# Macaron block in float32: turning the feed-forward tokens with VectorE's 32x32 blocks and DMAs by way of DRAM instead of TensorE transposes

## The chip, the cores and the metric

The kernel runs on one core of a Trainium2 chip. Its time is the device time of one execution in microseconds, given as the median of several runs. Profiles are of one execution, taken by the hardware profiler. The engines are TensorE (PE, with its weight loads PEld), VectorE (DVE), ScalarE (ACT), GpSimd (POOL) and SyncE (SP, which here only issues DMAs). Each engine works through its own instructions in program order and waits on semaphores for the others.

## The reference

```python
def reference(x, Wq, Wk, Wv, Wo, w1, b1, w2, b2):        # x: 16 x 256 x 256, float32
    x = x + 0.5 * ffn(layernorm(x), w1, b1, w2, b2)
    x = x + attention(layernorm(x), Wq, Wk, Wv, Wo)       # 16 heads of 16, rotary, causal
    x = x + 0.5 * ffn(layernorm(x), w1, b1, w2, b2)
    return x

def ffn(x, w1, b1, w2, b2):                               # 256 -> 1024 -> 256
    h = gelu(x @ bit_quant(w1).T + b1)                    # exact GELU
    return h @ bit_quant(w2).T + b2                       # bit_quant: round(w / mean|w|) to -1, 0, 1
```

## The kernel before

The 4096 tokens stay on the chip in eight tiles `x_0` to `x_7`, each a block of 512 tokens: 128 partitions, four tokens on each (`BT = 4`), 256 features. The program has three parts: the first feed-forward (`ln == 0`), the attention, whose first steps begin beside the first feed-forward's last blocks (`head`), and the last feed-forward (`ln == 2`), which begins beside the attention's end. Both feed-forwards are made by `ffn(ln, after)`.

A feed-forward works in 64 steps, `u = 8 i + f`, for block `i` and eighth `f` of the 1024 hidden features. Step `(i, f)` does `up(i, f)`: four matmuls of 512 columns into a PSUM tile `m`, two with the high part of the normalized tokens (`xnT[i][0]`) and then two with the rest (`xnT[i][1]`), each for two halves `k` of the 256 features. ScalarE then makes the GELU of `m` twice, once rounded to the matmul's format (`h_high`) and once whole (`h_whole`), and the difference `h_rest` is taken by GpSimd for f = 1, 3, 5 and by VectorE otherwise. The second product, `down`, is two steps behind (`LATE = 2`): step `u` ends with `down` of step `u - 2`, eight matmuls into a PSUM tile `w`, which want `h_high` and `h_rest` of that step. So after `up(i, 2)` TensorE does `down(i, 0)`, `up(i, 3)`, `down(i, 1)`, `up(i, 4)`, `down(i, 2)`. After a block's last `down` VectorE adds the product to `x` in two halves (this falls into step 1 of the next block); in the last feed-forward SP then stores the block.

The next block's tokens are made ready in between. `stats` takes mean and variance of the tokens of block `i + 2` on VectorE in steps 4 to 7, `finish_stats` makes `rstd` of them on GpSimd behind step 7. `prepare(i + 1)` in step 3 normalizes the next block's four token groups on VectorE into `xn`, of which there is one buffer. `turn_in(i + 1, k)` in steps 5 and 6 transposes them on TensorE, four 128x128 transposes per half `k` into a PSUM tile `mm`; ScalarE copies that to the high part, and VectorE subtracts it from the PSUM tile to get the rest. `add_bias(i)` in step 6 adds the output bias to `x_i` on GpSimd. In the first feed-forward, statistics for the attention's norm (`later`) are spread over the steps of the next block.

The order of every engine's instructions is the order in which the program writes them: the wrapper `InOrder` keeps it, so nothing is reordered by a planner. In the profile almost all instructions carry that wrapper's line, L172, so tiles tell them apart: `m` is up's product, `w` down's, `mm` what else goes through PSUM, `xnT` both the high part and the rest. `flat1` and `flat2` hold the raw weights `w1` and `w2` at first; later the attention's rotary step uses `flat1` and the first half of `flat2`.

Of the kernel before, what the change touches and what calls it, by code (L numbers as in the profile page):

```python
# [8 lines left out]
FP = mybir.dt.float32  # L9
FR = mybir.dt.float32r  # L10
AF = mybir.ActivationFunctionType
# [4 lines left out]
P = 128  # L16
D = 256
KC = D // P
FF = 1024
# [10 lines left out]
def kernel(  # L30
# [17 lines left out]
    BT = 4  # L48
    TB = BT * P
    NBLK = NT // TB  # L50
# [24 lines left out]
    b1_sb = const.tile([P, NFC], FP, name="b1_sb")  # L75
# [5 lines left out]
    flat1, flat2 = (state.tile([P, 2 * FF], FP, name=f"w_{n}") for n in range(2))  # L81
# [19 lines left out]
    for k in range(KC):  # L101
        rows = slice(k * P, (k + 1) * P)
        nc.sync.dma_start(out=wv[:, k, :], in_=wqkvT[rows, 2 * D :])
        for at in range(0, 2 * D, 4 * HD):
            n, j, e = at // D, at // P % 2, at // (4 * HD) % 2
            nc.sync.dma_start(
                out=wqk[:, k, n, j, :, e, :],
                in_=wqkvT[rows, at : at + 4 * HD].rearrange("p (r d) -> p r d", d=HD),
            )
    for at in range(0, P, HD):  # L110
        r, n = at // 32, at // HD % 2
        nc.sync.dma_start(
            out=wo[at : at + HD, :, :],
            in_=woT.rearrange("(k n r d) f -> n r d k f", n=2, r=4, d=HD)[n, r],
# [19 lines left out]
        out=mask_k,  # L134
        in_=mask_k,
# [28 lines left out]
    class InOrder:  # L164
# [11 lines left out]
    tensor, vector, scalar, gpsimd, sync = (  # L176
        InOrder(engine) for engine in (nc.tensor, nc.vector, nc.scalar, nc.gpsimd, nc.sync)
    )
# [4 lines left out]
    def stats(ln, n):  # L183
        st = small.tile([P, 6], FP, name="st")
        vector.bn_stats(st, tokens(n))
        vector.bn_aggr(mv[ln][:, n, :], st)

    def finish_stats(ln, first, n):

        var = small.tile([P, BT], FP, name="var")  # L190
        gpsimd.tensor_scalar(
            var[:, 0:n], mv[ln][:, first : first + n, 1], LN_EPS, 1.0, ALU.add, ALU.mult
        )
        gpsimd.tensor_tensor(
            rstd[ln][:, first : first + n], var[:, 0:n], power[:, 0:n], ALU.pow
        )

    def normalize(ln, n, to, engine=None):
        (engine or vector).tensor_scalar(
            to,  # L200
            tokens(n),
            mv[ln][:, n, 0:1],
            rstd[ln][:, n : n + 1],
            ALU.subtract,
            ALU.mult,
        )
# [68 lines left out]

    LATE = 2

    def ffn(ln, after):
        xn, xnT, hT, ys = {}, {}, {}, {}

        def measure(i):
            if ln == 0:
                for t in range(BT):
                    stats(0, i * BT + t)
                finish_stats(0, i * BT, BT)

        def prepare(i, engine=None):
            xn[i] = fp.tile([P, BT, D], FP, name="xn", bufs=1)
            for t in range(BT):
                normalize(ln, i * BT + t, xn[i][:, t, :], engine)  # L290
            xnT[i] = [fp.tile([P, KC, TB], FR, name=f"xnT_{n}") for n in range(2)]

        def add_bias(i):
            gpsimd.tensor_add(xs[i], xs[i], b2_sb.unsqueeze(1).to_broadcast([P, BT, D]))

        def turn_in(i, k):
            tp = ps_mm.tile([P, TB], FP, name="mm")
            for t in range(BT):
                tensor.transpose(
                    tp[:, t * P : (t + 1) * P], xn[i][:, t, k * P : (k + 1) * P], ident  # L300
                )
            high, rest = (xnT[i][n][:, k, :] for n in range(2))
            scalar.copy(high, tp)
            return lambda: vector.tensor_sub(rest, tp, high.bitcast(FP))

        first = {}

        def up_first(i, f, to=None):
            h = first[i, f] = ps_m.tile([P, TB], FP, name="m") if to is None else to
            for n in range(2):  # L310
                for k in range(KC):
                    tensor.matmul(
                        h,
                        w1q[:, k, f * P : (f + 1) * P],
                        xnT[i][n][:, k, :],
                        start=(n == 0 and k == 0),
                        stop=(n == 1 and k == KC - 1),
                    )

        def up(i, f):  # L320
            if (i, f) not in first:
                up_first(i, f)
            h = first.pop((i, f))
            high = fp.tile([P, TB], FR, name="h_high", bufs=LATE + 3)
            rest = fp.tile([P, TB], FR, name="h_rest", bufs=LATE + 3)
            whole = fp.tile([P, TB], FP, name="h_whole", bufs=3)
            scalar.activation(high, h, AF.Gelu, bias=b1_sb[:, f : f + 1])
            scalar.activation(whole, h, AF.Gelu, bias=b1_sb[:, f : f + 1])

            engine = gpsimd if f in (1, 3, 5) and not (ln == 0 and i == NBLK - 1) else vector  # L330
            engine.tensor_sub(rest, whole, high.bitcast(FP))
            hT[i, f] = (high, rest)

        def down(i, f):
            if f == 0 and ln == 2 and i == NBLK - 1:

                ys[i] = [ps_mm.tile([P, 2, D], FP, name="mm") for t in range(0, BT, 2)]
            elif f == 0:
                y = ps_w.tile([P, BT, D], FP, name="w")
                ys[i] = [y[:, t : t + 2, :] for t in range(0, BT, 2)]  # L340
            parts = hT.pop((i, f))
            order = [(t, n) for t in range(BT) for n in range(2)]
            if ln == 2 and (i, f) == (NBLK - 1, NFC - 1):

                order = [(t, n) for n in range(2) for t in range(BT)]
            for t, n in order:

                tensor.matmul(
                    ys[i][t // 2][:, t % 2, :],
                    parts[n][:, t * P : (t + 1) * P],  # L350
                    w2q[:, f, :],
                    start=(f == 0 and n == 0 and t % 2 == 0),
                    stop=(f == NFC - 1 and n == 1 and t % 2 == 1),
                )
            if f == NFC - 1:
                for t in range(0, BT, 2):
                    xt = xs[i][:, t : t + 2, :]
                    vector.scalar_tensor_tensor(
                        xt, ys[i][t // 2], 0.5, xt, ALU.mult, ALU.add
                    )  # L360
                for t in range(0, BT, 2):
                    after(i, t)

        def begin():
            measure(0)
            if ln == 0:
                sizes(0)
            prepare(0)
            if ln == 0:
                threshold(0)  # L370
                signs(0, lambda w: w[:, :, 0 : FF // 2])
            for k in range(KC):
                turn_in(0, k)()
            if ln == 0:
                signs(0, lambda w: w[:, :, FF // 2 :])
                sizes(1)

        def step(u):
            i, f = divmod(u, NFC)
            if i < NBLK:  # L380
                up(i, f)
                if ln == 0 and u == 0:
                    threshold(1)
                if ln == 0 and u in (0, 3):
                    part = slice(0, NFC // 2) if u == 0 else slice(NFC // 2, NFC)
                    signs(1, lambda w: w[:, part, :])
                if ln == 0 and u == 4:
                    gpsimd.tensor_scalar(b2_sb, b2_sb, 0.5, 0.0, ALU.mult, ALU.add)
                if u == 1:
                    measure(1)  # L390
                if f >= 4 and i + 2 < NBLK:
                    stats(ln, (i + 2) * BT + f - 4)
                    if f == NFC - 1:
                        finish_stats(ln, (i + 2) * BT, BT)
                if i + 1 < NBLK and (ln, i) != (2, 0):
                    if f == 3:
                        prepare(i + 1)
                    if f in (5, 6):
                        turn_in(i + 1, f - 5)()
                if f == (1 if i == NBLK - 1 else 6):  # L400
                    add_bias(i)
            if u >= LATE:
                down(*divmod(u - LATE, NFC))
            if ln == 0 and u == 2 * NFC + 2:
                make_tables()
            if ln == 0 and u < (NBLK - 1) * NFC and later:
                later.pop(0)()

        return begin, step, prepare, turn_in, up_first
# [14 lines left out]
    xn_a, xnT, qT, kT, o, oT, y_a = {}, {}, {}, {}, {}, {}, {}  # L424
# [307 lines left out]


    begin, step, prepare, turn_in, up_first = ffn(2, store)
    rest = []
    for p in range(8):
# [7 lines left out]
        rest = made  # L744
        if p == 0:
            prepare(0, gpsimd)
    a, z = NB - 2, NB - 1
# [84 lines left out]
```

## Time and profile before

| What | Value |
|---|---|
| Time, median of 3 runs | 620.18 us (618.72 to 620.56) |
| The profiled execution's own time | 619.01 us |
| Its span | 617.2 us |
| Granted TensorE clock | 0.999 |
| Busy: PE, DVE, ACT, POOL | 592.9, 475.6, 391.5, 322.2 us |
| DMA engines, mean over the span | 34 GB/s |
| First feed-forward | from about 8 to 141 us |
| Last feed-forward, steps | from about 480 us to the end |

The span is the profiled execution without what lies around it, some 1.8 us. Busy times are of this one execution; a matmul's end is modelled, so a busy PE is not PE at its peak. A line of the chain of waits gives start, duration and what the chain went through; a line of a timeline gives start, duration, engine, source line, operation, output and inputs with their shapes, and in brackets the idle time before it and who ended it.

### The profile page before, as it was taken

The page shows a single profiled execution, that of the slowest core. Times are in us where ns is not written, and L with a number is a line of the kernel's source. Part 1 is how long each engine was busy: PE and PEld are TensorE (multiplying, and loading weights), DVE is VectorE, ACT ScalarE, POOL GpSimd, SP SyncE. Part 2 cuts the span into 40 slices and gives each one's busy share as a digit, 9 for nine tenths or more (in the row PEclk, how much of TensorE's full clock was granted, in tenths as well). Part 3 has the DMA queues.
Part 4 walks back from the last instruction along what each step waited for, and adds up shares of the span by engine and source line. Part 5 has one row for each costly group of instructions (what it writes and reads, how often), then busy time and mean ns, then how long its engine had stood idle before and what let it go on. Part 6 is the DMA issues. An engine that isn't in the chain of part 4 may idle for free.

```text
span 617.2 us, 14403 instructions
## 1 busy us (share of the span) xinstructions
PE 592.9 (96%) x5388; PEld 471.5 (76%) x5388; DVE 475.6 (77%) x1682; ACT 391.5 (63%) x668; POOL 322.2 (52%) x297
## 2 busy tenths in 40 slices
PE   4999999999999999999999999999999999999997
PEld 3798989887667777777777777777766788888886
DVE  6877887786788888888889888888896466666653
ACT  4667666764576666565666666666665666666674
POOL 3655555682465556555665467453822354444443
PEclk9999999999999999999999999999999999999999
DMA  8810000000001001100010001100000011110001
GB/s 290 176 23 1 2 1 19 17 1 18 19 37 37 20 20 37 37 29 28 19 38 36 21 19 37 37 20 21 36 4 2 2 35 35 35 35 34 30 20 55
DMA packets 25589, 21.28 MB, mean 34 GB/s; under 512 B 11056, under 2 KB 21168, under 8 KB 25520
## 3 DMA queue, kind: packets, MB, share of 16 engines
q1 hardware_dynamic: 24960, 19.44, 9.9%
q8 instruction: 43, 0.70, 0.5%
q10 hardware_dynamic: 560, 0.92, 0.4%
q14 instruction: 26, 0.21, 0.1%
HBM read 7.51 MB, written 4.19 MB: 19 GB/s over the span
## 4 chain that ended last, share of the span: by engine, by line
PE 78%; DVE 12%; ACT 6%; issue 2%; DMA 1%; POOL 1%; DVEq 0%; SPq 0%; ACTq 0%; POOLq 0%
PE mm L172 29%; PE w L172 26%; PE m L172 23%; DVE masked L172 3%; DVE h_rest L172 2%; ACT pT L172 2%; DVE w L172 2%; ACT h_high L172 1%; ACT h_whole L172 1%; DMA w<-in_w1T_dram 1%; DVE xn L172 1%; DVE st L172 1%; DVE xnT L172 1%; DVE w2q L172 1%; DVE x L172 0%
## 5 line engine op out<-in xcount | busy, mean ns | idle before, releaser
L172 DVE CUSTOM_DVE_ANT_0 masked<-m,mask_q 128x128 f32<-128x128 f32 x480 | 141.8, 350 | 32.5 <-PE m L172 31.2
L172 PE MATMUL m<-xnT,w1q 128*128 128x512 f32 x504 | 142.5, 403 | 3.5 <-DVE xnT L172 2.7
L172 ACT ACTIVATE pT<-w 128x768 f32<-128x768 f32 x128 | 103.9, 812 | 65.9 <-DVE w L172 60.2
L172 ACT ACTIVATE h_high<-m,b_sb 128x512 fp32r<-128x512 f32 x126 | 86.8, 689 | 81.6 <-PE m L172 81.5
L172 PE MATMUL w<-qT,kT 32*128 32x256 f32 (+1 forms) x1024 | 126.3, 351 | 3.5 <-ACT pT L172 2.0
L172 DVE TENSOR_TENSOR h_rest<-h_whole,h_high 128x512 fp32r<-128x512 f32 x83 | 75.2, 908 | 68.0 <-ACT h_whole L172 67.7
L172 PE MATMUL m<-kT,qT 32*128 32x128 f32 x960 | 124.6, 352 | 0.7 <-ACT kT L172 0.7
L172 PEld LDWEIGHTS w<-qT,kT 32*128 32x128 f32 x1024 | 92.7, 184 | 38.4 <-issue 28.6
L172 PE MATMUL w<-w2q,h_high 128*128 128x256 f32 x480 | 120.8, 286 | 1.0 <-DVE w2q L172 1.0
L172 PE MATMUL w<-w2q,h_rest 128*128 128x256 f32 x480 | 118.1, 280 | 0.8 <-POOL h_rest L172 0.7
L172 POOL TENSOR_TENSOR h_rest<-h_whole,h_high 128x512 fp32r<-128x512 f32 x45 | 60.2, 1339 | 90.4 <-ACT h_whole L172 90.2
L172 PEld LDWEIGHTS m<-xnT,w1q 128*128 128x128 f32 x504 | 86.8, 190 | 19.1 <-DVE xnT L172 5.5
L172 PEld LDWEIGHTS w<-w2q,h_rest 128*128 128x128 f32 x480 | 90.6, 189 | 5.8 <-POOL h_rest L172 1.2
L172 PEld LDWEIGHTS w<-w2q,h_high 128*128 128x128 f32 x480 | 90.3, 188 | 5.6 <-DVE w2q L172 1.4
L172 DVE TENSOR_TENSOR w<-w,mask_k 128x512 f32<-128x512 f32 x128 | 88.9, 695 | 4.2 <-PE w L172 4.1
L172 ACT ACTIVATE h_whole<-m,b_sb 128x512 f32<-128x512 f32 x126 | 85.8, 681 | 0.0
L172 PEld LDWEIGHTS m<-kT,qT 32*128 32x128 f32 x960 | 73.2, 185 | 5.9 <-DVE maxes L172 4.1
L172 POOL TENSOR_TENSOR o<-avs,inv 128x256 f32<-128x256 f32 x32 | 20.3, 636 | 97.0 <-DVE inv L172 97.0
L172 PE MATMUL mm<-xnT_a,wqk 128*128 128x256 f32 x256 | 63.5, 391 | 0.0
L172 POOL TENSOR_TENSOR w<-w,cosT 128x512 f32<-128x512 f32 x32 | 41.3, 1289 | 30.0 <-ACT w L172 16.0
L172 POOL TENSOR_TENSOR w<-w,sinT 128x512 f32<-128x512 f32 x32 | 40.9, 1277 | 27.8 <-DMA w<-w 27.7
L172 PEld LDWEIGHTS mm<-xnT_a,wqk 128*128 128x128 f32 x256 | 46.1, 190 | 11.4 <-PE m L172 4.6
(86 smaller groups left out, 875.1 us busy)
## 6 DMA issues: line engine op xcount, KB each, us to landing
w<-w SPq DMA_DIRECT2D x64, 128.0 KB
out_dram<-x SPq DMA_DIRECT2D x15, 256.0 KB
x<-in_x_dram SPq DMA_DIRECT2D x7, 512.0 KB
w<-in_w2T_dram SPq DMA_DIRECT2D x1, 1024.0 KB
qT<-mT SPq DMA_DIRECT2D x64, 4.0 KB
w<-in_w1T_dram SPq DMA_DIRECT2D x1, 512.0 KB
w<-in_w1T_dram ACTq DMA_DIRECT2D x1, 512.0 KB
wqk<-in_wqkvT_dram SPq DMA_DIRECT2D x16, 32.0 KB
```

The lines of the kernel that those rows point to most:

```text
L172: return tc.keep_in_program_order(getattr(self.engine, name)(*args, **kwargs))
```

## The change

For blocks 2 to 7 of both feed-forwards (`by_blocks`) the tokens are no longer transposed on TensorE. `prepare` is moved from step 3 of the block before to its step 0. It normalizes as before, then VectorE transposes the block's 128x1024 values in 32x32 squares into `turned`, the second half of `flat2`; SP writes that to a DRAM tile of 512 KB (two buffers) and reads it back in four DMAs of 128 KB, each to 32 partitions of the rest's buffer `xnT[i][1]`, in pieces of 512 bytes. In step 6 `turn_in` copies both halves to the high part on ScalarE, out of SBUF, and then VectorE subtracts the high part from the rest in place.

The tokens of such a block stand in another order in the transposed layout. The GELU puts them back: its input is read in the new order and its two outputs are written in the old one, in runs of 32 columns.

`stats` and `finish_stats` of steps 4 to 7 are written behind `prepare` and `turn_in` in the step, no longer ahead of them. Block 1 is turned as before.

```diff
+    turned = flat2[:, FF:]
+    dram = ctx.enter_context(
+        tc.tile_pool(name="rows", bufs=2, space=bass.MemoryType.DRAM)
+    )
     def ffn(ln, after):
         xn, xnT, hT, ys = {}, {}, {}, {}
+        by_blocks = range(2, NBLK)
...
             xnT[i] = [fp.tile([P, KC, TB], FR, name=f"xnT_{n}") for n in range(2)]
+            if i in by_blocks:
+                vector.transpose(turned, xn[i].rearrange("p n (j t) -> p j n t", t=32))
+                rows = dram.tile([P, 2 * TB], FP, name="rows")
+                sync.dma_start(out=rows, in_=turned)
+                of = rows.rearrange("(a f) (k j q) -> j f k a q", a=4, k=KC, j=4)
+                for j in range(4):
+                    sync.dma_start(
+                        out=xnT[i][1][32 * j : 32 * j + 32]
+                        .bitcast(FP)
+                        .rearrange("p k (a q) -> p k a q", a=4),
+                        in_=of[j],
+                    )
...
         def turn_in(i, k):
+            if i in by_blocks:
+                high, rest = (xnT[i][n][:, k, :] for n in range(2))
+                scalar.copy(high, rest.bitcast(FP))
+                return lambda: vector.tensor_sub(rest, rest.bitcast(FP), high.bitcast(FP))
...
-            scalar.activation(high, h, AF.Gelu, bias=b1_sb[:, f : f + 1])
-            scalar.activation(whole, h, AF.Gelu, bias=b1_sb[:, f : f + 1])
+            for to in (high, whole):
+                if i in by_blocks:
+                    to = to.rearrange("p (n a t) -> p a n t", n=BT, a=4)
+                    of = h.rearrange("p (a n t) -> p a n t", n=BT, a=4)
+                else:
+                    of = h
+                scalar.activation(to, of, AF.Gelu, bias=b1_sb[:, f : f + 1])
...
                 if u == 1:
                     measure(1)
+                if i + 1 < NBLK and (ln, i) != (2, 0):
+                    early = i + 1 in by_blocks
+                    if f == (0 if early else 3):
+                        prepare(i + 1)
+                    if early and f == 6:
+                        for rests in [turn_in(i + 1, k) for k in range(KC)]:
+                            rests()
+                    if not early and f in (5, 6):
+                        turn_in(i + 1, f - 5)()
                 if f >= 4 and i + 2 < NBLK:
                     stats(ln, (i + 2) * BT + f - 4)
                     if f == NFC - 1:
                         finish_stats(ln, (i + 2) * BT, BT)
-                if i + 1 < NBLK and (ln, i) != (2, 0):
-                    if f == 3:
-                        prepare(i + 1)
-                    if f in (5, 6):
-                        turn_in(i + 1, f - 5)()
```

## The prediction

> **What bounds the kernel now.** I read the page first, then TensorE's share by stage, then the chain of waits over one block, then the timelines of VectorE (DVE) and GpSimd (POOL) beside it, then the spread of single durations by tile. "up" is the four matmuls of a step into `m`, "down" the eight into `w`.
>
> ```profile
> PE 592.9 (96%) x5388; PEld 471.5 (76%) x5388; DVE 475.6 (77%) x1682; ACT 391.5 (63%) x668; POOL 322.2 (52%) x297
> ```
> The stages (us, then busy us per engine), one block each, from the first feed-forward (FFN) and from the last:
> ```profile
> 63.21:79.01 15.80, 15.80 (x106) 14.27 (x105) 12.67 (x30) 11.08 (x19) 9.54 (x9) 1.00 0.01 2
> 528.78:545.41 16.63, 16.09 (x107) 14.20 (x106) 10.54 (x22) 11.09 (x19) 7.47 (x6) 1.00 0.10 33
> ```
> TensorE is all there is in the first; in the last it lacks 0.54 us a block. The chain over that block's end (start, us, what) shows why:
> ```profile
> 523.39 0.44 PE mm L172 x4
> 523.83 0.94 PE w L172 x8
> 524.77 0.94 PE m L172 x4
> ...
> 525.74 0.69 ACT h_high L172
> 526.42 0.59 ACT h_whole L172
> ...
> 527.04 1.96 DVE h_rest L172
> 528.99 0.35 DVE st L172
> ...
> 529.55 0.59 DVE xnT L172
> ...
> 530.18 0.50 PE m L172
> ```
> A step is 0.93 + 0.94 = 1.87 us, eight are 14.95; the two groups of four transposes (`mm`) add 0.88, the wait 0.5 to 0.8. The 1.96 us `h_rest` is what the prediction turns on. In the timeline:
> ```profile
> 526.02 2.42 POOL L172 TENSOR_TENSOR x<-x,b_sb 128x1024 f32<-128x1024 f32 x1
> ...
> 527.04 1.96 DVE L172 TENSOR_TENSOR h_rest<-h_whole,h_high 128x512 fp32r<-128x512 f32 x1 [1.14 <-ACT h_whole L172]
> ...
> 529.46 0.66 DVE L172 TENSOR_TENSOR xnT<-mm,xnT 128x512 fp32r<-128x512 f32 x1
> ```
> DVE's difference of two SBUF tiles stands still until POOL's bias add ends (528.44) and then needs 0.57 more. By tile (ns, min/median/max):
> ```profile
> L172 DVE TENSOR_TENSOR h_rest<-h_whole,h_high x83: 658/693/2843, 15.1 to 611.2; 128x512 fp32r<-128x512 f32 x83
> ...
> L172 DVE TENSOR_TENSOR xnT<-mm,xnT x32: 652/658/692, 11.5 to 595.4; 128x512 fp32r<-128x512 f32 x32
> ...
> L172 DVE STREAM_TRANSPOSE oT<-o x32: 433/435/446, 181.6 to 486.8; 128x256 f32<-128x256 f32 x32
> ```
> The same subtraction with one operand in PSUM (`xnT<-mm`) was never held, at most 692 ns. Normalizations (SBUF to SBUF) are held too; here the four of a block in DVE's timeline, and in POOL's the work among them:
> ```profile
> 70.53 2.33 DVE L172 TENSOR_SCALAR xn<-x,mv,rstd 128x256 f32<-128x256 f32 x4
> ```
> ```profile
> 71.28 1.43 POOL L172 TENSOR_TENSOR h_rest<-h_whole,h_high 128x512 fp32r<-128x512 f32 x1 [2.44 <-ACT h_whole L172]
> ```
> Undisturbed the four take 1.38 (as at 536.36); POOL cut in ahead of the last one, which waited out the whole 1.3 us.
>
> **What is removed.** 2 x 4 transposes on TensorE in twelve block ends (blocks 2 to 7 of both FFNs): 0.88 each. If nothing else were late, all blocks would go to 14.95: 0.86 off 15.81 in the first FFN, 1.66 off 16.61 in the last.
>
> **What is added.** (a) DVE: one 128x1024 block transpose per block. `oT` (256 columns) takes 0.435, `avs` (512, out of PSUM) 0.707, so 1.06 ns a column: 1.25 us; between 0.9 (if the fixed part is larger) and 1.5 (if the 32-column runs cost), I take 1.25. None of the 32 `oT` was held (446 ns at most), so I take it as free of POOL. (b) Each rest is now SBUF minus SBUF: 0.60 as before, but now open to POOL's hold. (c) ACT's copy reads SBUF, 0.59 as from PSUM (`vals`, written in strided runs, takes 372 ns and the plain `mT` 371, so the turned GELU output costs nothing; bounds 0 and 0.1, hidden in ACT's 0.6 us idle per step). (d) SP: five DMAs. The wait for the first one's landing stands ahead of the stores, which nobody awaits, and in blocks 5 and 6 ahead of the rotary pairs.
>
> The trip: two stores of 256 KB give the price, SP's timeline first, then what the DMA engines moved in slices of 0.1 us from 534 on.
> ```profile
> 534.31 0.97 SPq L728 DMA_DIRECT2D out_dram<-x  x2
> ```
> ```profile
> GB/s 0 0 0 0 0 0 0 0 0 0 0 0 236 358 369 317 287 338 379 328 338 348 358 348 358 358 348 154 21 0 0 0 0 0 0 0 0 0 0 0
> ```
> First byte 0.9 after issue, 512 KB in 1.5, and 0.4 until the semaphore is acted on (a rotary pair's last data at 157.05 released POOL at 157.54): 2.8 us out. Back: four issues at 0.5 (bounds 0.37, a store, and 0.95, the `wqk` loads), 0.5 to the last one's first byte, 0.4 of data, 0.45 to act: 3.35. Together 6.1; with the dear issues 8. The 64-byte pieces of `wqk` moved at some 60 GB/s (8.7 us for 512 KB), which sets the upper end at 15; 512-byte pieces lie nearer to the store's 1 KB. The Trainium skill ("DMA: Bandwidth & Descriptors", Anatomy of one DMA) puts about 2 us of fixed cost on each DMA, most of it the write receipt, longest towards HBM; an estimate by that is 3.2 out and 4.7 back, 7.9. No row here shows a store's receipt that long, and the sum below would not change.
>
> **The timetable of a changed block, last FFN.** Zero is the end of up(i,0). An `h_rest` can start 1.33 after its up (530.68 to 532.01). DVE's r1, the second rest, ends 0.55 before zero (530.13 to 530.68). Behind it now come statistics 0.53, h_rest(7) 0.60, statistics 0.53: 1.11. `var` and `rstd` on POOL take 1.39 (531.27 to 532.66): 2.50. h_rest(0) is done at 1.93, so the normalizations, moved to step 0, wait for rstd, start at 2.55, and meet POOL's h_rest(1), ready at 1.87 + 1.33 = 3.20: two pass, POOL runs to 4.54, two follow to 5.20. Block transpose to 6.4. The residual adds of the block before (2 x 0.60) stand behind it: 7.6. Then h_rest(2) meets POOL's h_rest(3) (5.61 + 1.33 = 6.94, to 8.23) and ends at 8.23 + 0.57 = 8.80. TensorE wants it for down(2) at 4 x 1.87 = 7.48: a new wait of 1.37, where before DVE had 0.9 us of idle time in front of it.
>
> Everything behind moves by 1.37: h_rest(5) on POOL from 9.35 + 1.37 + 1.33 = 12.05 to 13.3, the bias add to 15.7. h_rest(6), ready at 11.22 + 1.37 + 1.33 = 13.92, is held to 15.7 and ends at 16.3; two rests make 17.5; plus 0.55 the next zero is 18.04. Without this second wait it would be 14.95 + 1.37 = 16.32. So 18.04 against 16.61. The trip isn't in it: transposed at 6.4, landed at 12.5; DVE wants the copies from 16.3 on, so landing may be 3 us later.
>
> **First FFN.** The same up to 8.80 (one statistics more fits under POOL's hold). `rstd` of the attention norm stands ahead of the bias add, which asks at 13.3 + 1.4 = 14.7. DVE does h_rest(6) 13.92 to 14.52 and r0 to 15.15; POOL, waiting, goes next (as in the rows at 71.28) until 17.57; r1 ends 18.14, zero at 18.69 against 15.81: +2.9. If r1 came first the block would be about 16.4, but h_rest(7) would be held instead, and rstd would reach the next block at +4.3, which lengthens the wait at down(2) to 2.0: 16.4 to 18.7 are the bounds. Blocks 5 and 6 run beside the attention's first steps. In block 5 TensorE has 4.8 us of projections between its steps, under which both waits mostly fit: +0.5 (bounds -0.9, +2.9). In block 6 the rotary products on POOL meet the normalizations (already 3.4 us of chain there, 123.62): +2.8 (bounds -0.9, +5).
>
> The Trainium skill ("VectorE: DVE Perf Modes", What auto-detection actually checks) lets an op with one SBUF source use both ports; the `oT` rows show neither that speed nor a hold. By that rule the block transpose would take some 0.7, as an estimate, and h_rest(2) behind it would still be held to 8.80.
>
> **Sum.** First FFN 4 x 2.9 + 0.5 + 2.8 = 14.9. Last FFN: its first changed block takes 16.02 now, so 2.0, then 5 x 1.43 = 7.2: 9.2. Together +24.1. The profiled execution took 619.01 (span 617.2), 1.2 under the median of 620.18; on the median, 644.
>
> **Rivals.**
> (1) The hold doesn't reach the new forms, or POOL's bias add comes after all three differences, and nothing stalls: 4 x 0.86 + 0.9 + 1.5 in the first FFN, 1.07 + 5 x 1.66 in the last, 15 off: 604. Its place is step 6; it decides if the bias add asks after r1 has started, 0.4 us later than in the first FFN's undelayed order (9.35 + 1.33 + 1.3 + 1.4 = 13.4) and 1.8 later in the last. For it: 0.9 us of idle DVE before h_rest(2) today. Against it: every bias add in the last FFN's rows holds h_rest(6).
> (2) The four normalizations keep POOL out, so the wait at down(2) vanishes (transposed at 5.1, h_rest(2) at 6.9, before POOL asks) and only the bias add costs: last FFN 14.95 + 1.4 = 16.35 (-1.0 in sum), first FFN about 17.3 (+6.9 with blocks 5 and 6): 626. Against it: the 2.33 row.
> (3) The trip is the limit: from landing later than 15.5 on, each us is one per block. At the 64-byte rate landing is near 19: up to 3.8 x 12 on top, half of it likelier: 667.
>
> **Chances.** Forecast 0.66, (2) 0.15, (3) 0.09, (1) and mixtures that come out faster 0.10. A measurement here tells 0.3% (1.9 us) from no change; of (2), 0.03 lies within that. So faster 0.10, same 0.03, slower 0.87. The range leaves out (1) and (3): from 621, the low end of (2), to 662, the forecast with block 6 at +5, block 5 at +2.9 and half a us more in each block and wait.
>
> **What would show it.** Right: in the last FFN's blocks a period near 18.0 with two gaps on TensorE, before down(2) on `h_rest` and before up(i+1,0) on `xnT`; `xnT` differences on DVE with maxima above 1.5 us; `rstd` about 2.5 after zero; copies on ACT not waiting for DMA. Wrong: `xnT<-xnT` never over 0.75 us (then 1), blocks with one gap only (2), or ACT's copies released by a DMA (3).

## The result and the profile after

The changed kernel takes 648.37 us (median of 4 runs, 647.78 to 649.25) against 619.62 us before (618.72 to 620.56): the ratio is 1.0465, 95% interval 1.0443 to 1.0487. The prediction was 644 (621 to 662), so the direction, the size and most of the mechanism held; the first feed-forward cost more than forecast.

The profiled execution has a span of 646.9 us (before 617.2), 29.7 more. First the page's line of busy times, the granted clock in tenths, and the chain that ended last, by engine:

```profile
PE 595.4 (92%) x5292; PEld 467.5 (72%) x5292; DVE 510.1 (79%) x1694; ACT 393.1 (61%) x668; POOL 323.7 (50%) x297
...
PEclk9998989889999999999999999999999999999999
...
PE 56%; DVE 22%; DMA 6%; ACT 5%; issue 5%; POOL 3%; SPq 2%; DVEq 0%; ACTq 0%; POOLq 0%
```

TensorE has 96 instructions fewer and is nevertheless busy 2.5 us longer. One part of that is its clock, which was halved for a while in the first feed-forward (the 8s in the clock's row; more on that at the end). Another is that a block broken up by waits shows more busy time even at full clock: 15.87 us in the last feed-forward's row below, against 14.93 where nothing waits (e9). It was on 78% of the chain before and is on 56% now. VectorE's busy time grew by 34.5 us: twelve block transposes are 15 of that, and most of the rest is operations that stand still while GpSimd works. The page's groups say what TensorE waited for (after the bars: busy us, mean ns of one, then idle us just before them and what ended most of it):

```profile
L172 PE MATMUL m<-xnT,w1q 128*128 128x512 f32 x504 | 151.0, 415 | 16.3 <-DVE xnT L172 14.2
...
L172 PE MATMUL w<-w2q,h_rest 128*128 128x256 f32 x480 | 121.8, 286 | 16.1 <-DVE h_rest L172 14.6
```

Before, those two idle times were 3.5 and 0.8 us. These are the two waits the prediction named: the next block's tokens (`xnT`) before `up(i+1, 0)`, and `h_rest` before `down`. One block of each feed-forward in the view by stages (columns as in the prediction's):

```profile
551.00:569.25 18.25, 15.87 (x97) 13.41 (x96) 13.47 (x23) 10.98 (x19) 7.83 (x7) 1.00 0.26 88
64.00:83.00 19.00, 15.65 (x100) 13.57 (x99) 15.50 (x32) 11.16 (x19) 9.52 (x9) 1.00 0.17 56
```

The periods, from one block's fourth matmul of `up(i, 0)` to the next block's, tell where the 29.7 us are. In the table, block i's period is the one in which block i + 1 is made ready, so the change acts on blocks 1 to 6:

| Block | 1 | 2 | 3 | 4 | 5 | 6 | sum |
|---|---|---|---|---|---|---|---|
| First FFN, before | 15.81 | 16.87 | 15.81 | 15.82 | 20.61 | 17.19 | 102.1 |
| First FFN, after | 17.13 | 19.17 | 18.99 | 18.96 | 24.04 | 23.30 | 121.6 |
| Last FFN, before | 16.72 | 16.61 | 16.62 | 16.62 | 16.61 | 16.08 | 99.3 |
| Last FFN, after | 18.34 | 18.24 | 18.24 | 18.21 | 18.25 | 18.25 | 109.5 |

That is +19.5 and +10.3, together the whole difference of the spans. VectorE's timeline over one block of the last feed-forward, with GpSimd's beside it, shows both waits being made (start, duration, operation; in brackets the idle time before it):

```profile
549.19 2.37 DVE L172 TENSOR_TENSOR h_rest<-h_whole,h_high 128x512 fp32r<-128x512 f32 x1 [3.52 <-ACT h_whole L172]
551.48 1.28 DVE L172 TENSOR_TENSOR xnT<-xnT,xnT 128x512 fp32r<-128x512 f32 x2
...
556.26 2.40 DVE L172 TENSOR_SCALAR xn<-x,mv,rstd 128x256 f32<-128x256 f32 x4 [0.91 <-POOL rstd L172]
558.70 1.25 DVE L172 STREAM_TRANSPOSE w<-xn 128x1024 f32<-128x1024 f32 x1
559.87 1.25 DVE L172 SCALAR_TENSOR_TENSOR x<-w,x 128x512 f32<-128x512 f32 x2
561.04 1.79 DVE L172 TENSOR_TENSOR h_rest<-h_whole,h_high 128x512 fp32r<-128x512 f32 x2
```
```profile
548.61 2.40 POOL L172 TENSOR_TENSOR x<-x,b_sb 128x1024 f32<-128x1024 f32 x1
554.55 0.20 POOL L172 TENSOR_SCALAR var<-mv 128x4 f32<-128x4 f32 x1 [3.54 <-DVE mv L172]
554.83 1.40 POOL L172 TENSOR_TENSOR rstd<-var,power 128x4 f32<-128x4 f32 x1
556.58 1.30 POOL L172 TENSOR_TENSOR h_rest<-h_whole,h_high 128x512 fp32r<-128x512 f32 x1 [0.35 <-ACT h_whole L172]
560.32 1.28 POOL L172 TENSOR_TENSOR h_rest<-h_whole,h_high 128x512 fp32r<-128x512 f32 x1 [2.45 <-ACT h_whole L172]
```

(The block transpose's target `turned` carries the name `w` in the trace, after the weights that lay there first.) At 549.19 `h_rest(6)` stands still until GpSimd's bias add ends at 551.01, then needs 0.55, and only then do the two rests of `xnT` follow: the wait at the block's end. From 556.26 on, the normalizations, the block transpose and the residual adds are one queue, and it is itself lengthened by a hold: the four normalizations take 2.40 us where four undisturbed ones took 1.38, with GpSimd's `h_rest(1)` (556.58) among them; `h_rest(2)` begins behind it at 561.04, is held by GpSimd's `h_rest(3)` to 561.60 and reaches TensorE at 562.2: the wait before `down(i, 2)`. In TensorE's row of steps the first wait makes a step of 3.41 out of 1.87 (1.54 lost), the second 3.50 (1.63 lost).

### The profile page after: what moved, and what is told of

It is laid out like the page before. It is cut to its first block, busy times and chain, and to the rows that moved or that the text cites. A ratio compares the mean times of both kernels' runs of the same rounds, so it can differ in the third digit from the quotient of the medians.

```text
span 646.9 us, 14484 instructions
## 1 busy us (share of the span) xinstructions
PE 595.4 (92%) x5292; PEld 467.5 (72%) x5292; DVE 510.1 (79%) x1694; ACT 393.1 (61%) x668; POOL 323.7 (50%) x297
## 4 chain that ended last, share of the span: by engine, by line
PE 56%; DVE 22%; DMA 6%; ACT 5%; issue 5%; POOL 3%; SPq 2%; DVEq 0%; ACTq 0%; POOLq 0%
PE mm L172 26%; PE w L172 17%; PE m L172 13%; DVE xnT L172 4%; DMA xnT<-rows 4%; DVE w L172 4%; DVE xn L172 4%; DVE h_rest L172 3%; DVE masked L172 2%; SPq L172 2%; POOL rstd L172 2%; ACT pT L172 2%; DMA rows<-w 2%; DVE st L172 1%; DVE x L172 1%
## 5 line engine op out<-in xcount | busy, mean ns | idle before, releaser
L172 PE MATMUL m<-xnT,w1q 128*128 128x512 f32 x504 | 151.0, 415 | 16.3 <-DVE xnT L172 14.2
L172 PE MATMUL w<-w2q,h_rest 128*128 128x256 f32 x480 | 121.8, 286 | 16.1 <-DVE h_rest L172 14.6
L172 DVE TENSOR_TENSOR h_rest<-h_whole,h_high 128x512 fp32r<-128x512 f32 x83 | 77.7, 936 | 66.7 <-ACT h_whole L172 66.6
L172 PEld LDWEIGHTS m<-xnT,w1q 128*128 128x128 f32 x504 | 89.4, 194 | 37.9 <-DVE xnT L172 22.1
L172 PEld LDWEIGHTS w<-w2q,h_rest 128*128 128x128 f32 x480 | 92.5, 193 | 24.9 <-DVE h_rest L172 18.1
L172 PEld LDWEIGHTS w<-w2q,h_high 128*128 128x128 f32 x480 | 92.5, 193 | 6.8 <-DVE w2q L172 1.5
```

The lines of the kernel that those rows point to most:

```text
L172: return tc.keep_in_program_order(getattr(self.engine, name)(*args, **kwargs))
```

## The experiments

All ran beside the kernel before on the same chips; ratios are to that kernel. "Step" is the distance from one `up` to the next on TensorE, 1.87 us when nothing waits. A, B and C are the theories named in the expectations: holds and queue on VectorE, the trip by DRAM, and the plain load.

### e1: no bias add

```diff
-                if f == (1 if i == NBLK - 1 else 6):
-                    add_bias(i)
```

> The changed kernel without the bias add on GpSimd (the output bias is left out). Three theories. A, holds: GpSimd's operations hold VectorE's SBUF operations at two places of each block, before down(2) and behind the bias add, and the trip by DRAM stands little behind them. B, trip: the 8.0 us trip sets the block's end. C, load: VectorE has too much to do, 1.25 us of block transpose per block on top. A: the hold of step 6 goes, but the trip is next. In the last feed-forward h_rest(6) can start at 13.9 after zero instead of being held to 16.3, the copies come with the landing (transposed at 6.4, plus 8.0 is 14.4), rests at 15.0 to 16.2, zero at 16.8, and as the statistics come earlier too, blocks of 16.8 to 17.8 instead of 18.24: 3 to 9 us off; in the first feed-forward 1.1 to 2 us off each of six blocks, 7 to 12. In sum 10 to 20 off, 628 to 638. B: at most 0.4 per block, 643 to 648. C: no change, 645 to 648.

Measured: 628.83 us (626.85 to 630.93), ratio 1.0150 (1.0122 to 1.0178). In the last feed-forward the step of 3.41 before `down(2)` stays, the end step shrinks from 3.50 to 2.1 to 2.9, and a block takes 16.8 to 17.6 (blocks 2 to 6; block 1, at 15.0, has next to no wait). No `h_rest(6)` is held any more, and none of the half-clock windows occurs. Taking the bias add away is worth 19.5 us (the kernel before pays for its bias add too, so this is not all the change's doing; e7 estimates that share). What is late next shows in VectorE's timeline of e1:

```profile
567.30 0.69 DVE L172 TENSOR_TENSOR h_rest<-h_whole,h_high 128x512 fp32r<-128x512 f32 x1 [3.54 <-ACT h_whole L172]
568.96 1.29 DVE L172 TENSOR_TENSOR xnT<-xnT,xnT 128x512 fp32r<-128x512 f32 x2 [0.97 <-ACT xnT L172]
```

The rests now wait 0.97 for ScalarE's copies, which wait for the trip.

### e2: no trip by DRAM

```diff
-                rows = dram.tile([P, 2 * TB], FP, name="rows")
-                sync.dma_start(out=rows, in_=turned)
...
+                half = turned[:, k * TB : (k + 1) * TB]
+                scalar.copy(high, half)
+                return lambda: vector.tensor_sub(rest, half, high.bitcast(FP))
```

> The changed kernel without the five DMAs: ScalarE and VectorE read the block transpose's result in SBUF, so the tokens of blocks 2 to 7 of both feed-forwards are in a wrong order. Everything else stands. A (holds): the last feed-forward's blocks stay at 18.2 with the same two waits, since the copies are not what VectorE waits for (h_rest(6) is held to 16.3 anyway); the first one's lose at most 0.5 each. In sum 0 to 4 off: 644 to 648. B (trip): the end of each block comes 2 us earlier or more, 12 times: 625 or less. C (load): no change.

Measured: 650.63 us (648.86 to 651.5), ratio 1.0498 (1.0476 to 1.0520). Without any of the 60 DMAs the last feed-forward's blocks keep 18.22 to 18.34 us. The trip was not what set the time, although the chain of waits gave DMA 6% of the span. The chain ran through the DMA because ScalarE's copies began 0.60 us late by it:

```profile
567.99 1.14 ACT L172 CAST xnT<-xnT 128x512 fp32r<-128x512 f32 x2 [0.60 <-DMA xnT<-rows]
```

But VectorE, held on `h_rest(6)` to 569.8, could not have used the copy before that. Two paths ended 0.7 us apart, and removing the one that the view had followed brought nothing. In the first feed-forward e2 was slower in block 6 (26.24) and had more half-clock windows; that part decides nothing.

### e3: neither bias add nor trip

Both edits of e1 and e2.

> Neither the bias add nor the five DMAs (output bias left out, tokens of blocks 2 to 7 in a wrong order). A (holds): the wait before down(2), 1.4 to 1.5, is all that is left over 14.95, so blocks of 16.4 in both feed-forwards: 12 x 2 off in sum, with blocks 5 and 6 a little less: 620 to 628. More than the two runs with one part each add up to, if the one part hides behind the other. B (trip): as without the trip alone, 625 or less, and no further gain from the bias add. C (load): 645 to 648.

Measured: 624.92 us (624.39 to 626.82), ratio 1.0092 (1.0071 to 1.0113). Blocks 2 to 6 of the last feed-forward take 16.53 to 16.57 (block 1 14.93), with the 3.41 step before `down(2)` as the only one above 1.95. From e1 to e3 the blocks gain 0.3 to 1.1 us: the trip is the limit that comes next when the hold is gone.

### e4: no block transpose on VectorE

```diff
-                vector.transpose(turned, xn[i].rearrange("p n (j t) -> p j n t", t=32))
...
-                sync.dma_start(out=rows, in_=turned)
+                sync.dma_start(out=rows, in_=xn[i].rearrange("p n d -> p (n d)"))
```

> The changed kernel without VectorE's block transpose: the first DMA reads the normalized tokens themselves, so the features of blocks 2 to 7 come out unturned. The 1.25 us on VectorE are gone, the rest stands, the trip starts 1.25 earlier. A (holds): the residual adds end at 6.4, so h_rest(2) starts before GpSimd's h_rest(3) asks at 6.94 and is done at 7.0, ahead of its 7.48: the whole first wait (1.54) goes, the second stays. Last feed-forward 16.6 to 16.8 per block, 6 x 1.5 = 9 off; first feed-forward 0.2 to 1.6 per block, 1 to 8 off: 631 to 638. B (trip): 1.25 per block, 15 off: 633; the first wait stays. C (load): 1.25 x 12 = 15 off, spread over both waits: 633. The chain tells A from B and C: the wait before down(2) gone (A) or there (B).

Measured: 632.55 us (630.62 to 633.76), ratio 1.0202 (1.0174 to 1.0230). Taking 1.25 us per block off VectorE removes the whole wait before `down(2)` in the last feed-forward (step 1.87 again, 2.06 in block 1) and leaves the end step at 3.50 (blocks 16.69). VectorE's timeline says how: `h_rest(2)` now runs ahead of GpSimd's `h_rest(3)`, unheld, and `h_rest(6)` is held as before.

```profile
567.31 0.68 DVE L172 TENSOR_TENSOR h_rest<-h_whole,h_high 128x512 fp32r<-128x512 f32 x1
...
573.40 2.37 DVE L172 TENSOR_TENSOR h_rest<-h_whole,h_high 128x512 fp32r<-128x512 f32 x1 [1.96 <-ACT h_whole L172]
```

Per block the time falls by 1.55, more than the 1.25 removed: queue and hold go together. Block 5 of the first feed-forward falls from 24.04 to 19.81, below the 20.61 of before.

### e5: `h_rest(3)` on VectorE

```diff
-            engine = gpsimd if f in (1, 3, 5) and not (ln == 0 and i == NBLK - 1) else vector
+            engine = gpsimd if f in (1, 5) and not (ln == 0 and i == NBLK - 1) else vector
```

> The changed kernel with one more difference on VectorE: h_rest(3) of every block is taken by VectorE instead of GpSimd, so nothing of GpSimd runs when h_rest(2) comes up. VectorE gets 0.6 us more work per block. Holds: h_rest(2) follows the residual adds at 7.6 and ends at 8.2 instead of 8.8, so the wait before down(2) falls from 1.54 to about 0.8 and the last feed-forward's blocks from 18.24 to 17.4 to 17.6; the end of the block stays. In sum 4 to 5 off in the last, 2 to 5 in the first: 638 to 643. Load: more work on VectorE, so the waits grow by 0.6 per block, 12 x 0.6 = 7 on top: 655; or, if the first wait is only a queue, no change in it, 648.

Measured: 646.31 us (642.59 to 647.65), ratio 1.0426 (1.0384 to 1.0469), which misses the expected 638 to 643. The step before `down(2)` goes from 3.41 to 3.00 in blocks 2 to 6 of the last feed-forward, so the hold by `h_rest(3)` is 0.4 of the 1.54. The other 1.1 is the queue ahead of `h_rest(2)`: I had put too much on that one hold. But 1.0 of this queue is a hold as well, that of the four normalizations by `h_rest(1)`, which e5 leaves in place. What happens where it is absent can be seen in VectorE's timeline of e1, block 1 and then block 2 of the last feed-forward:

```profile
506.41 1.38 DVE L172 TENSOR_SCALAR xn<-x,mv,rstd 128x256 f32<-128x256 f32 x4
...
522.29 2.41 DVE L172 TENSOR_SCALAR xn<-x,mv,rstd 128x256 f32<-128x256 f32 x4 [0.91 <-POOL rstd L172]
```

The step before `down(2)` is 1.87 in the first of these blocks and 3.41 in the second. The same holds wherever the block transpose stands in step 0 (the changed kernel, e1, e2, e3, e5, e6 and e10): the step is 1.87 in all 19 blocks whose normalizations took 1.4, and 2.99 or more in every block where they were held, 2.36 or more, but one (block 2 of the changed kernel's first feed-forward, which begins at half clock). This doesn't isolate the hold. In 10 of the 19 the normalizations also started 0.8 earlier in the block, and the other 9 begin with TensorE at half clock, so that it wants `h_rest(2)` later. No run takes this hold away alone.

### e6 and e7: the bias add two steps earlier

The same edit in the changed kernel (e6) and in the kernel before (e7):

```diff
-                if f == (1 if i == NBLK - 1 else 6):
+                if f == (1 if i == NBLK - 1 else 6 if (ln, i) == (0, 0) else 4):
```

> The changed kernel with the bias add of a block in step 4 instead of step 6 (but in the first feed-forward's block 0). GpSimd does it between h_rest(3) and h_rest(5), where it idled. Holds: as without the bias add, since h_rest(6) and the rests meet nothing: last feed-forward's blocks 16.9 instead of 18.24. It holds h_rest(4) instead, from 8.8 to 10.65 + 0.57 = 11.2, and down(4) wants that at 11.22 or, after the wait before down(2), later. 626 to 632. Load: no change, 648.

> The kernel before (tokens turned on TensorE) with the bias add in step 4 instead of step 6. Holds: the 1.96 us h_rest(6) of the last feed-forward falls to 0.69 and the wait for the last rest with it: blocks of 15.8 instead of 16.6, 4 to 5 off in sum; the first feed-forward, which has no wait there, stays within 0.4 per block either way: 613 to 618. If the hold is not what made TensorE wait there, no change: 619.5.

Measured, e6: 635.65 us (634.46 to 637.13), ratio 1.0266 (1.0243 to 1.0290). In the last feed-forward it does what e1 did (blocks 2 to 6 at 16.84 to 17.85, block 1 at 15.14); it misses its range because blocks 5 and 6 of the first feed-forward stay at 23.3 and 23.92. e7: 617.22 us (616.61 to 620.37), ratio 0.9979 (0.9964 to 0.9993). There the last feed-forward's blocks fall from 16.61 to 15.81 to 15.82 each, the 0.8 us that the bias add cost the kernel before; blocks 5 and 6 of the first feed-forward, at 21.85 and 20.8 (from 20.61 and 17.19), lengthen by about as much. So some 4.4 of e1's 19.5 us (99.3 less 94.9 over the last feed-forward's six blocks; an estimate, as e7 moves the bias add and e1 leaves it out) were lost already before the change.

### e8: prepared two blocks ahead

```diff
-            xnT[i] = [fp.tile([P, KC, TB], FR, name=f"xnT_{n}") for n in range(2)]
+            xnT[i] = {1: fp.tile([P, KC, TB], FR, name="xnT_1", bufs=3)}
...
+                if i + 1 in by_blocks and i + 1 < NBLK and f == 5:
+                    for rests in [turn_in(i + 1, k) for k in range(KC)]:
+                        rests()
+                if i + 2 < NBLK:
+                    first_f = 4 if (ln, i) == (0, 0) else 0
+                    if 0 <= f - first_f < BT:
+                        stats(ln, (i + 2) * BT + f - first_f)
+                        if f - first_f == BT - 1:
+                            finish_stats(ln, (i + 2) * BT, BT)
+                    if f == (7 if (ln, i) == (0, 0) else 6):
+                        prepare(i + 2)
+                halves = {2: (0, 2), 4: (2, 4)}
...
+                if f in halves:
+                    add_bias(i, *halves[f])
```

> A version made of the findings. Tokens of blocks 2 to 7 are turned by VectorE and DMAs, but two blocks ahead: statistics of block i + 2 in steps 0 to 3 of block i, normalizing, block transpose and DMAs behind h_rest(6) of step 6, when GpSimd is idle, ScalarE's copies and the rests in step 5 of block i + 1, half a block after the landing. The buffer of the rests is threefold for it. The bias add is split in two halves of 1.25 us, in steps 2 and 4. Holds: nothing that TensorE wants soon meets GpSimd: blocks near 14.95 + 0.1 in both feed-forwards but where the attention's first steps run: 15 off the kernel before, 603 to 610. Trip: landed long before it is used, the same. Load: VectorE still has the 1.25 us and everything else, so blocks of 16.5 and more: 618 or above.

Measured: 613.87 us (613.21 to 614.08), ratio 0.9912 (0.9897 to 0.9927): 0.9% faster than the kernel before, with every operation of the change still in it. Blocks 2 to 6 of the last feed-forward take 15.41 to 15.45 (block 1 14.93). It misses its range for two reasons in the trace: step 1 of each of these blocks is 2.34 to 2.39, with `h_rest(7)` behind the block transpose in VectorE's queue, and block 1 of the first feed-forward takes 20.59. There an `h_rest` stands behind normalizations that waited 1.42 for `rstd` and behind the block transpose, and is then held by a half of the bias add (1.70 us at 36.26); TensorE waits 2.63 us for it and then runs 6.8 us at half the clock.

### e9: the same, with the queue in another order

```diff
-        by_blocks = range(2, NBLK)
+        by_blocks = range(3 if ln == 0 else 2, NBLK)
...
+                if i + 2 in by_blocks:
+                    if f == 6:
+                        prepare(i + 2)
+                    if f == 7:
+                        turn_blocks(i + 2)
```

> Edit: e8's order two blocks ahead, with two things changed: the block transpose and its DMAs go from step 6 to step 7, behind h_rest(7) on VectorE (the normalizations stay at step 6), and block 2 of the first feed-forward is turned on TensorE in steps 5 and 6 of block 1, so that nothing is prepared two ahead in block 0. Theory A (VectorE's queue and holds set the remaining waits): in e8 a last-FFN block took 15.41 to 15.45, of it 0.48 because h_rest(7) stood behind the block transpose, and block 1 of the first FFN 20.59 because VectorE was late by the rstd it waited for in block 0. Both go: last-FFN blocks near 14.95 (14.93 to 15.1), first-FFN block 1 near 15.8, and 613.9 becomes 613.9 - 11 x 0.48 - 4.8 + 0.9 for the eight transposes that TensorE does again = 604.7 (602 to 608). Theory C (the plain load on VectorE, the extra 1.25 us a block, is what costs): the order inside the queue makes no difference, last-FFN blocks stay at 15.4, and only block 1 of the first FFN gains: 609 to 612.

Measured: 606.92 us (605.23 to 607.47, 5 runs), ratio 0.9800 (0.9782 to 0.9818), inside the 602 to 608 of theory A; C's 609 to 612 is out. Every block of the last feed-forward takes 14.93 us, TensorE's own time, and blocks 3 and 4 of the first do too. VectorE is busy for 80% of the span, no less than in the changed kernel, but has 9% of the chain in place of 22%:

```profile
PE 581.5 (96%) x5300; PEld 463.4 (77%) x5300; DVE 482.1 (80%) x1693; ACT 391.7 (65%) x668; POOL 324.6 (54%) x310
...
PEclk9999999999999999999999999999999999999999
...
PE 77%; DVE 9%; POOL 5%; ACT 4%; issue 2%; DMA 1%; DVEq 0%; SPq 0%; ACTq 0%; POOLq 0%
```

The load on VectorE was not the cost; what it stood in front of was. That is near rival (1)'s number, 604, reached by another order. Not all of the gain over the kernel before is the transposes' doing: of the 1.68 us that a block of the last feed-forward lost (16.61 to 14.93), e7 puts 0.8 on the moved bias add, and the eight transposes are the other 0.88.

### e10: block 7 of the first feed-forward on TensorE

```diff
-        by_blocks = range(2, NBLK)
+        by_blocks = range(2, NBLK - 1 if ln == 0 else NBLK)
```

> Edit: the changed kernel, but block 7 of the first feed-forward is transposed on TensorE as in the kernel before (by_blocks ends at 6 there); all else as changed. The theory on block 6 (its four normalizations, waiting for rstd in step 0, alternate with the rotary products on GpSimd, 5.32 us instead of 1.4, and everything behind them on VectorE is late): with the normalizations back at step 3 and no block transpose there, block 6 of the first FFN goes from 23.3 to 17.2 to 18.5, and block 5 stays at 24.0; the time is 648.4 - 5.5 = 642.9 (641 to 644.5). The rival (block 6 is slow because block 5 ends late, or by the half clock): block 6 stays above 21 and the time above 646.

Measured: 643.66 us (642.26 to 644.21), ratio 1.0394 (1.0376 to 1.0412), as the theory had it. Block 6 falls from 23.30 to 17.80. Why it was slow stands in the changed kernel's timelines of VectorE and GpSimd:

```profile
132.96 5.32 DVE L172 TENSOR_SCALAR xn<-x,mv,rstd 128x256 f32<-128x256 f32 x4 [0.91 <-POOL rstd L172]
138.31 1.25 DVE L172 STREAM_TRANSPOSE w<-xn 128x1024 f32<-128x1024 f32 x1
```
```profile
132.90 1.29 POOL L172 TENSOR_TENSOR w<-w,sinT 128x512 f32<-128x512 f32 x1
134.26 1.29 POOL L172 TENSOR_TENSOR w<-w,w 128x512 f32<-128x512 f32 x1
135.52 1.31 POOL L172 TENSOR_TENSOR h_rest<-h_whole,h_high 128x512 fp32r<-128x512 f32 x1
136.79 1.34 POOL L172 TENSOR_TENSOR w<-w,cosT 128x512 f32<-128x512 f32 x1
138.09 1.34 POOL L172 TENSOR_TENSOR h_rest<-h_whole,h_high 128x512 fp32r<-128x512 f32 x1
```

Four normalizations of 0.35 us each take turns with GpSimd's products of 1.3: 5.32 us for 1.4 us of work, at the head of a queue that TensorE's `h_rest(2)` stands in. In e10 the normalizations stand in step 3 and still take 4.70 us (rows not shown), and TensorE waits 1.8 in that step, 1.4 in the changed kernel; but the step before `down(2)` falls from 6.33 to 1.87 and the one at the end from 4.0 to 1.87, against 0.9 for the transposes on TensorE. Part of the 6.33 is the half clock: the awaited `h_rest` came at 141.9, just as the clock was halved (141.92), and the matmuls behind it in that step took some 1.5 us longer than elsewhere (0.21 between two of `down` in place of 0.12, and 1.71 for an `up` in place of 0.93). That window is absent in e10.

Block 5 fell too, from 24.04 to 22.62, which I had not expected. VectorE's queue is the same there in both (an `h_rest` of 1.75 behind GpSimd's product), but in the changed kernel the clock was halved from 118.03, when that `h_rest` ended, and the step is 6.00 against 4.67.

## Why the prediction was right, and where its numbers were off

**The hold, confirmed.** The prediction's centre was that a difference of two SBUF tiles stands still on VectorE while GpSimd works on SBUF, and that the change opens `xnT` to that. By tile (ns, min/median/max):

```profile
L172 DVE TENSOR_TENSOR xnT<-xnT,xnT x24: 677/679/2881, 44.8 to 625.0; 128x512 fp32r<-128x512 f32 x24
...
L172 DVE TENSOR_TENSOR xnT<-mm,xnT x8: 653/680/687, 11.5 to 496.8; 128x512 fp32r<-128x512 f32 x8
L172 DVE STREAM_TRANSPOSE w<-xn x12: 1245/1246/1247, 35.2 to 613.4; 128x1024 f32<-128x1024 f32 x12
```

The form out of PSUM is still never held; the new form is, up to 2.88 us, in the first feed-forward, where the forecast had r1 held by the bias add. The block transpose costs 1.246 us every time (forecast 1.25, by the columns of `oT`) and is never held, also where GpSimd worked all through it (138.31, in e10's rows). The 0.7 that the prediction estimated by the Trainium skill ("VectorE: DVE Perf Modes", What auto-detection actually checks) did not come. That section makes the rule depend on firmware enabling the mode for the instruction, which the prediction left out.

**The last feed-forward, right.** The forecast period was 18.04, measured 18.24. Its terms: wait before `down(2)` 1.37, measured 1.54; wait at the block's end 1.72, measured 1.63; the remaining 0.1 is a first step of 1.98. `h_rest(2)` ended 8.84 after zero (forecast 8.80), although `rstd` came at 2.9 and not at 2.50: it took 1.40 here and 1.02 in the rows that I had summed. The 0.4 was covered, because the end of `h_rest(3)` on GpSimd set the end of `h_rest(2)`: that this error did not show is luck. Of the first wait's 1.54, 0.4 is the hold by `h_rest(3)` (e5) and 1.1 the queue, of which 1.0 is the hold of the normalizations; the forecast's timetable had both. The sum, 9.2, measured 10.3. Two of its inputs do not hold: 8.80 less 7.48 is 1.32, not 1.37, and no block took the 16.02 from which it reckoned the first changed one (16.72 in the table; the last took 16.08). With the table's periods the same 18.04 gives 9.0.

**The first feed-forward, low by 4.6.** Blocks 1 to 4 were put at +2.9 each, 11.6; measured +1.32, +2.30, +3.18 and +3.14, 9.9. The bias add did hold r1, as forecast: the last step of these blocks is 4.00 to 4.26, so 2.1 to 2.4 lost (forecast 18.69 - 16.32 = 2.37). The wait before `down(2)` is there in block 3 alone (1.64). In block 1 the normalizations were not held (1.38 us), and blocks 2 and 4 begin at half clock. The terms that were mis-sized most are blocks 5 and 6:

- Block 5: +0.5 forecast, +3.4 measured. The step that failed is "both waits mostly fit" under the projections. The wait before `down(2)` falls into a step without projections. VectorE's queue there holds the attention's normalizations (`xn_a`) as well, and GpSimd holds those and `h_rest` (rows below the list). Without the block transpose the wait is gone (e4, 19.81). With it the wait is also gone in e2 and e5 (21.39 and 21.47), where the block's normalizations met nothing of GpSimd (1.38 us; 2.37 here) and the block began at half clock. About 1.3 of the +3.4 is the half clock.
- Block 6: +2.8 forecast, +6.1 measured. The mechanism (rotary products against the normalizations) was named, and e10 fits it, but it was sized by the 3.4 us chain of the kernel before; it was 5.32 here, one product for each normalization. That lies above the forecast's upper bound of +5. About 1.5 of it is the half clock.

Block 5's rows, from VectorE's timeline and then from GpSimd's:

```profile
114.81 1.76 DVE L172 TENSOR_SCALAR xn_a<-x,mv,rstd 128x256 f32<-128x256 f32 x2
116.49 1.75 DVE L172 TENSOR_TENSOR h_rest<-h_whole,h_high 128x512 fp32r<-128x512 f32 x1
```
```profile
115.14 1.28 POOL L172 TENSOR_TENSOR h_rest<-h_whole,h_high 128x512 fp32r<-128x512 f32 x1 [4.05 <-ACT h_whole L172]
116.38 1.31 POOL L172 TENSOR_TENSOR w<-w,cosT 128x512 f32<-128x512 f32 x1
```

So some 2.8 us of the excess of these two blocks, 6.2 over the forecast, came from a term that the sum did not have at all: the clock, full in every stage of the kernel before, was taken as given.

**The trip, mis-sized without effect.** From the block transpose's end (559.95) to the copies' release (567.9) it took 8.0 us, not 6.1. SP's timeline:

```profile
559.97 0.34 SPq L172 DMA_DIRECT2D rows<-w  x1
560.75 0.93 SPq L761 DMA_DIRECT2D out_dram<-x  x2
563.12 2.53 SPq L172 DMA_DIRECT2D xnT<-rows  x4
```

Out it took 3.2 (forecast 2.8, with 0.4 for the semaphore where the row that it cites gives 0.49); back 4.8 (forecast 3.35): the four issues took 2.53 instead of 2.0, and from the end of the last one to the release it took 2.3 instead of 1.35. The estimate by the Trainium skill ("DMA: Bandwidth & Descriptors", Anatomy of one DMA), 3.2 and 4.7, was nearer than my sum from the stores' rows, although that section is about DMAs that GpSimd issues and these go out from SP. Nor do the two stores wait behind the landing, as the forecast said: they are issued ahead of the four reads. The sign "copies on ACT not waiting for DMA" failed as well: they waited 0.60 us for the landing in the block of the rows above. The prediction had taken such a wait for the sign of rival (3), and it was not. None of this moved the period (e2), because VectorE was held longer; e3 against e1 shows that it would count in a kernel without the hold.

**The rivals.** (1), no hold: the hold is there, in every block end. (2), only the bias add costs: the wait before `down(2)` is there in the last feed-forward, so no: the normalizations did not keep GpSimd out (2.40 us, with `h_rest(1)` among them). e4 shows the 1.25 us by which that wait decides. (3), the trip as the limit: e2 says no.

## What to carry to other kernels

When work moves from a full engine to one with idle time, write out the receiving engine's queue in order, with what every waiting consumer stands behind: here 1.25 us a block on an engine that was 77% busy cost 1.5 us a block, and the same work, placed where nothing due soon stood behind it, cost TensorE no wait (e9, 2% faster than the kernel before, part of it by the moved bias add). Ask of each operand whether it moved from PSUM to SBUF, because that opened it to GpSimd's hold. And do not read a share of the chain of waits as what its removal would bring: a second path ended 0.7 us behind the DMA's.

## What the runs showed of the hardware that I had not expected

**The clock falls after a partly idle window.** In the first feed-forward TensorE's granted clock was halved for 3.41 us at 49.76, 87.31, 118.03 and 141.92, always on one grid of 3.41 us. The view by windows, each pair being a window of the grid and the one after it (length, then busy us of PE, PEld, DVE, ACT, POOL, then the clock):

```profile
46.35:49.76 3.41, 1.41 (x10) 1.37 (x11) 3.38 (x5) 1.01 (x3) 1.40 (x1) 1.00 0.00 0
49.76:53.17 3.41, 3.41 (x14) 3.00 (x13) 2.27 (x7) 1.66 (x3) 1.96 (x3) 0.50 0.02 5
63.41:66.83 3.42, 2.14 (x14) 1.57 (x12) 3.42 (x3) 2.21 (x4) 3.42 (x2) 1.00 0.00 0
66.83:70.24 3.41, 2.72 (x18) 2.49 (x19) 2.96 (x7) 1.58 (x3) 1.00 (x3) 1.00 0.00 0
```

In the changed kernel the four windows with 1.41 us or less of TensorE work were each followed by one at half clock, and none with 2.03 or more was. Over all twelve profiles, of the windows at full clock every one with up to 1.51 us was followed by half clock (19 cases), from 1.52 to 1.97 some were (4), and from 2.02 on none. An idle time of 2 us is enough if it falls inside one window. The Trainium skill ("TensorE: Matmul & The Clock Gate", What's actually happening) puts the fall after an idle window of about 3.4 us; here the window was not idle, only 40% busy. Such a window costs up to 1.7 us of TensorE's work, but not always time: in blocks 2 and 4 of the first feed-forward the slower TensorE no longer had to wait before `down(2)`, and they took about as long as block 3, which had no half clock. In blocks 5 and 6 it came on top.

**The hold works both ways, even on a tiny operation.** `rstd`, 128x4 on GpSimd, takes 1.02 us, and 1.40 in five of six blocks of the last feed-forward of the changed kernel, where VectorE's `h_rest` (554.65 to 555.34, next to the 554.83 of the POOL rows above) has just begun (in the sixth nothing of VectorE runs beside it, and it takes 1.03). Where `h_rest` begins after `rstd`, neither is longer: at 517.91 in e9, `rstd` takes 1.02 and `h_rest`, beginning 0.17 later, 0.69. The Trainium skill ("SBUF — State Buffer", Who interferes with whom) says that a VectorE operation with two inputs in SBUF contends with a GpSimd instruction that reads SBUF; the first of these cases agrees, and in the second the small GpSimd operation, though begun first, held nothing.
